# Self-attention of a fused transformer block: the shift of half of the scores moved from DMAs to VectorE and GpSimd, and a reciprocal taken on turned squares

## The chip, the cores and the metric

The program runs on one core of a Trainium2 chip. The metric is the device time of one execution in microseconds (us). Three runs of the kernel before gave a median of 2473.12 us (2465.09 to 2479.93).

The engines are named as in the profile: PE is TensorE (matmuls), PEld its weight loads, DVE is VectorE, ACT is ScalarE, POOL is GpSimd, SP is SyncE, which here only issues DMAs. SBUF is the on-chip memory and PSUM the memory into which matmuls write.

## The reference

A block of eight batches with 512 rows of 512 numbers goes through a cross-attention layer, then through a block of self-attention, a second cross-attention and an MLP. All is float32. Only the self-attention is touched here; it has 16 heads of width 32, and its queries and keys both have 512 positions:

```python
x_norm = modulate(_ln(x), shift_a, scale_a)
qkv = x_norm @ W_qkv + b_qkv
q, k, v = jnp.split(qkv, 3, axis=-1)
...
attn_w = jax.nn.softmax(jnp.einsum('bhqd,bhkd->bhqk', q, k) * scale, axis=-1)
attn_out = jnp.einsum('bhqk,bhkd->bhqd', attn_w, v)
...
attn_out = attn_out @ W_proj + b_proj
x = x + gate_a[:, None] * attn_out
```

## The kernel before

The program runs its stages one after the other: a setup, the first cross-attention (phase "x"), the self-attention (`self_phase`, phase "a", from about 430 us to about 1315 us of the profiled span), the second cross-attention ("c") and the MLP ("m"). In these stages every engine works through its instructions in the order in which the program lists them; no scheduler reorders them. So the place of a call in the loop is its place in the queue of its engine.

**Groups.** The self-attention works in 32 groups. One group is four heads of one batch: eight batches (`b`) times four sets of heads (`fc`, 0 to 3). A group holds its scores turned: keys lie on the 128 partitions and queries along the row, so a group has four key tiles `k` of 128 keys, each with four heads of 512 queries. Each key tile is held as two SBUF tiles `e[k][0]` and `e[k][1]` of 128 x 1024 numbers, two heads in each.

**The steps of one group**, with the lines of the profile:

- `scores(k)`: eight matmuls (L1177) write two PSUM tiles `sT`. ACT copies both into `e[k]` (L1195). DVE keeps a running maximum `mx` over the key tiles (L1197, two instructions for each of k = 1, 2, 3), which also reads PSUM. The PSUM tiles have two buffers, so the matmuls of tile k+1 wait until both readers of tile k are through.
- `maxima()`: DVE turns each of the four heads' maxima in 32 x 32 squares (L1208) and reduces them (L1209), into `part`.
- `spread()`: PE turns `part` (L1217), DVE reduces it to the negated maximum of every query and head (L1221), and SP stores these 8 KB to DRAM as `mxd` (L1226).
- `shift(k)`: two DMAs for each key tile (L1231), issued by POOL, read a row of `mxd` for all 128 partitions and add it to `e[k][0]` and `e[k][1]` on the way.
- `exp(k)`: ACT takes the exponent in place (L1240).
- `add_up(k)`: adds `e[k]` into `sum`, on POOL for k = 1 and 2, on DVE for k = 3 (L1247).
- `outputs(k)`: matmuls with the values (L1257) accumulate in PSUM.
- `total()` and `finish()`: PE sums over the partitions with a matrix of ones (L1268), so that `z_ps` holds the sum of each head in all of the 32 partitions that belong to it. DVE takes the reciprocal of all 128 x 512 numbers (L1275) and multiplies the output by it (L1278).

**The loop.** The steps of three groups are interleaved: in the round of group `g`, its successor `nxt` has its scores and maxima computed, `prev` has its last tiles finished and the group before that (`past`) is divided. `beside(b, fc)` gives each round four pieces of eight matmuls, `f[0]` to `f[3]`, made of queries, keys, values or the output projection of this or a neighbouring batch (L352, L360). DVE also does, in the rounds where they are due, the bias of the projection (`res_a`, L1145) and the statistics of the next layer norm (L253 and L254 in rounds fc = 3, L268 to L298 in rounds fc = 0). `flush` puts on POOL the product of a projected tile with its gate (L1148) and the DMA that adds it to the residual in DRAM (L1151).

The order of one round is therefore, for PE: scores 0, the turned maxima of `g`, the sums of `past`, `f[0]`, scores 1, outputs 2 of `prev`, `f[1]`, scores 2, outputs 3 of `prev`, half of `f[2]`, scores 3, its other half, outputs 0 of `g`, `f[3]`, outputs 1 of `g`. In round fc = 2 there are four more small pieces that turn x (L1098).

Of the kernel before, what the change touches and what calls it, by code (L numbers as in the profile page):

```python
# [11 lines left out]
F32 = mybir.dt.float32  # L12
I32 = mybir.dt.int32
AF = mybir.ActivationFunctionType
ALU = mybir.AluOpType
# [4 lines left out]
P = 128  # L20
# [10 lines left out]
def tile_pixart_block(ctx: ExitStack, tc: tile.TileContext, a: dict, out: bass.AP):  # L31
    nc = tc.nc
    x, ctx_in, cond = a["x"], a["ctx_1024"], a["cond_1024"]
    B, N, _ = x.shape
# [13 lines left out]
    small = ctx.enter_context(tc.tile_pool(name="small", bufs=4))  # L48

    def load_w(name, u, rows=False, pool=wpool, queue=nc.sync):  # L50

        t = pool.tile([P, KC, H], F32, tag="w", name=f"w_{name}_{u}")
        w = a[name]
        src = w[ts(u, H), :] if rows else w[:, ts(u, H)]
        queue.dma_start(out=t, in_=src.rearrange("(k p) f -> p k f", p=P))
        return t
# [135 lines left out]
    with tc.tile_pool(name="setup_ps", bufs=4, space=PSUM) as spp, tc.manual_schedule(  # L192
# [6 lines left out]
        for name, n in col_names:  # L199
            at = col_at[name]  # L200
            nc.gpsimd.dma_start(
                out=brow[at : at + n, :],
                in_=a[name][0 : n * P].rearrange("(c p) -> c p", p=P),
# [193 lines left out]
    with tc.tile_pool(name="ps_s", bufs=2, space=PSUM, reuse_waits="tile") as ps_s:  # L397
# [672 lines left out]
        def self_phase(w, bo_row, work, work_2, ctx_c):  # L1070
# [6 lines left out]
            SQ = 32  # L1077
            KQ = N // SQ
# [6 lines left out]
            def flush(part):  # L1085

                while later[part]:
                    later[part].popleft()()
# [6 lines left out]
            def transpose_x(b, k):  # L1095
                pt = ps_m.tile([P, H], F32, tag="m", name=f"lnT_ps_a{b}_{k}")
                for t in range(NT):
                    nc.tensor.transpose(pt[:, ts(t, P)], x_cur[:, t, ts(k, P)], ident)  # L1098
                o = work.tile([P, N], F32, tag="xnT", bufs=5, name=f"xnT_a{b}_{k}")
                nc.scalar.activation(  # L1100
                    o, pt, AF.Identity,
                    bias=mod_l1[:, k, b : b + 1], scale=mod_l1[:, KC + k, b : b + 1],
                )
                st[b]["xT"].append(o)
# [54 lines left out]
            class Group:  # L1159
# [53 lines left out]
                def spread(self):  # L1213


                    pt = ps_m.tile([P, H], F32, tag="m", name=f"mxT_ps_{self.nm}")
                    nc.tensor.transpose(  # L1217
                        pt[: 4 * KQ, :P], self.part.rearrange("p h c -> p (h c)"), ident
                    )
                    row = small.tile([4 * KQ, SQ], F32, tag="mxT", bufs=1, name=f"mxT_{self.nm}")  # L1220
                    nc.vector.tensor_reduce(  # L1221
                        row, pt[: 4 * KQ, :P].rearrange("c (g q) -> c q g", q=SQ), AX.X, ALU.max,
                        negate=True,
                    )
                    self.mxd = dram.tile([4, N], F32, tag="mx", bufs=4, name=f"mxd_{self.nm}")
                    nc.sync.dma_start(out=self.mxd.rearrange("h (c q) -> (h c) q", q=SQ), in_=row)  # L1226

                def shift(self, k):

                    for i in range(2):  # L1230
                        nc.gpsimd.dma_start(  # L1231
                            out=self.e[k][i].rearrange("p h n -> p (h n)"),
                            in_=self.mxd[2 * i : 2 * i + 2, :]
                            .rearrange("h n -> (h n)").partition_broadcast(P),
                            accum_op=ALU.add,
                        )

                def exp(self, k, halves=(0, 1)):
                    for i in halves:
# [32 lines left out]

                def finish(self):
                    r = work.tile([P, N], F32, tag="rz", bufs=1, name=f"rz_{self.nm}")
                    nc.vector.reciprocal(r, self.pz)  # L1275
                    o = work.tile([P, N], F32, tag="oT", bufs=6, name=f"oT_{self.nm}")
                    st[self.b]["o"].append(o)
                    return nc.vector.tensor_tensor(o, self.po, r, ALU.mult)  # L1278

            def beside(b, fc):  # L1280

                more = b + 1 < B
                none = iter(())
                if fc == 0:
                    return [values(b, 2), values(b, 3), queries(b, 2), keys(b, 2)]
                if fc == 1:
                    done = [project(b - 1, t) if b else none for t in range(2)]
                    return [queries(b, 3), done[0], keys(b, 3), done[1]]
                done = [project(b - 1, t) if b else none for t in (2, 3)]
                if fc == 2:  # L1290
                    return done + ([queries(b + 1, 0), keys(b + 1, 0)] if more else [none, none])
                return [values(b + 1, 0), values(b + 1, 1), queries(b + 1, 1), keys(b + 1, 1)]
# [20 lines left out]
            for n, g in enumerate(groups[:-1]):  # L1313
                b, fc = g.b, g.fc
                nxt = groups[n + 1]
                more = b + 1 < B
                f = beside(b, fc)
                turning = fc == 2 and more
                if fc == 3:
                    ln = normalise_x("a", b + 2, True) if b + 2 < B else iter(())  # L1320
                if not more and fc == 1:
                    ctx_c.w_k = load_w("L1_xcond_W_kvc", 0)
                if prev is not None:
                    prev.outputs(1)
                nxt.scores(0)
                g.spread()
                if past is not None:
                    past.total()
                    past.finish()
                if prev is not None:  # L1330
                    prev.add_up(2, [0])
                g.shift(0)
                if prev is not None:
                    prev.add_up(2, [1])
                    prev.exp(3, [0])
                for k in range(1, NT):
                    g.shift(k)
                flush(0)
                flush(1)
                if fc == 1 and more:  # L1340
                    next(ln)
                pump(f[0], 4)
                nxt.scores(1)
                if fc == 3 or (b, fc) == (0, 0):
                    next(ln, None)
                    next(ln, None)
                elif fc == 0 and more:
                    next(ln)
                if turning:
                    transpose_x(b + 1, 0)  # L1350
                if prev is not None:
                    prev.exp(3, [1])
                    prev.outputs(2)
                if fc == 1 and more:
                    next(ln)
                pump(f[1], 4)
                if fc == 1 and not more:
                    ctx_c.load()
                    ln = ctx_c.norm()
                if turning:  # L1360
                    transpose_x(b + 1, 1)
                nxt.scores(2)
                if turning:
                    transpose_x(b + 1, 2)
                if fc == 2 and not more:
                    next(ln)
                    next(ln)
                if prev is not None:
                    prev.add_up(3)
                if (b, fc) == (0, 0):  # L1370
                    next(ln)
                if prev is not None:
                    prev.outputs(3)
                if turning:
                    transpose_x(b + 1, 3)
                    if b + 2 < B:
                        load_x(b + 2)
                flush(0)
                flush(1)
                g.exp(0)  # L1380
                pump(f[2], 2)
                nxt.scores(3)
                pump(f[2], 2)
                g.exp(1)
                g.add_up(1)
                if fc == 2 and not more:
                    run(ln)
                nxt.maxima()
                g.outputs(0)
                pump(f[3], 4)  # L1390
                if fc == 2 and not more:
                    ctx_c.transpose()
                g.exp(2)
                past, prev = prev, g

            g = groups[-1]
# [6 lines left out]
            prev.exp(3)  # L1403
            for k in range(1, NT):
                g.shift(k)
            flush(0)
            flush(1)
            prev.outputs(2)
# [99 lines left out]
        with tc.tile_pool(name="work_a", bufs=2, reuse_waits="tile") as work, tc.tile_pool(  # L1508
            name="ps_a", bufs=2, space=PSUM, reuse_waits="tile"
        ) as ps_m, tc.tile_pool(  # L1510
            name="ps_o", bufs=2, space=PSUM, reuse_waits="tile"
# [28 lines left out]
    with tc.tile_pool(name="mlp", bufs=1, reuse_waits="tile") as mlp, tc.tile_pool(  # L1540
        name="mlp_w", bufs=MC // KC - 1, reuse_waits="tile"
    ) as mlp_w, tc.tile_pool(
        name="ps_q", bufs=6, space=PSUM, reuse_waits="tile"
    ) as ps_q, tc.tile_pool(
        name="ps_t", bufs=2, space=PSUM, reuse_waits="tile"
# [39 lines left out]
        SQ = 32  # L1585
# [216 lines left out]
        for c in range(2):  # L1802
            g, r, s = [mlp.tile([P, H2], F32, tag="xr", bufs=4, name=f"shift_{i}_{c}")[:B] for i in range(3)]
# [47 lines left out]
```

## Time and profile before

| | |
|---|---|
| median of 3 runs | 2473.12 us (2465.09 to 2479.93) |
| profiled execution | 2467.43 us, of which the span of the engines is 2465.6 us |
| busy over the span | PE 95%, PEld 61%, DVE 68%, ACT 47%, POOL 52% |
| TensorE clock granted, mean | 0.984 |
| busy from 909 to 1011 us (102 us, most of one batch of the self-attention) | PE 98.71, DVE 86.46, ACT 74.30, POOL 75.80 us |
| share of the 16 DMA engines in that stretch | 0.97, 187 GB/s |
| DMAs that shift the scores (L1231) | 256 of 512 KB, 11.6 us median from issue to landing |
| reciprocal of the sums (L1275) | 32 on DVE, 3357 ns each |

A row of a timeline gives the start in us, the duration, the engine, the line, the operation with output and inputs, the shape, the number of instructions merged into the row, and in brackets the idle time of the engine before it with what ended it. A matmul of 512 float32 columns appears as two instructions. POOL rows can overlap: an instruction's row may begin while DMA descriptors ahead of it on POOL are still being written.

### The profile page before, as it was taken

The page shows a single profiled execution, that of the slowest core. Times are in us where ns is not written, and L with a number is a line of the kernel's source. Part 1 is how long each engine was busy: PE and PEld are TensorE (multiplying, and loading weights), DVE is VectorE, ACT ScalarE, POOL GpSimd, SP SyncE. Part 2 cuts the span into 40 slices and gives each one's busy share as a digit, 9 for nine tenths or more (in the row PEclk, how much of TensorE's full clock was granted, in tenths as well). Part 3 has the DMA queues.
Part 4 walks back from the last instruction along what each step waited for, and adds up shares of the span by engine and source line. Part 5 has one row for each costly group of instructions (what it writes and reads, how often), then busy time and mean ns, then how long its engine had stood idle before and what let it go on. Part 6 is the DMA issues. An engine that isn't in the chain of part 4 may idle for free.

```text
span 2465.6 us, 44805 instructions
## 1 busy us (share of the span) xinstructions
PE 2344.2 (95%) x17737; PEld 1508.8 (61%) x17737; DVE 1665.7 (68%) x2861; ACT 1168.7 (47%) x2045; POOL 1271.8 (52%) x1325
## 2 busy tenths in 40 slices
PE   8889998899999999999988899998999999999998
PEld 4667776323333333333324677777888888888887
DVE  3677774588888888888755787767555546555552
ACT  1456663577677777777653566642122121121120
POOL 2467774367786777867664567755302312213122
PEclk9899999999999999999999799999999999999999
DMA  7456666498999999999995224433422322223210
GB/s 247 128 130 145 123 131 117 89 189 171 193 191 182 197 173 194 192 181 180 201 205 148 78 64 89 80 70 104 89 40 60 73 53 64 58 54 78 44 51 26
DMA packets 145848, 300.94 MB, mean 122 GB/s; under 512 B 17573, under 2 KB 48437, under 8 KB 145125
## 3 DMA queue, kind: packets, MB, share of 16 engines
q0 software_dynamic: 60192, 176.24, 40.3%
q1 hardware_dynamic: 80148, 111.33, 15.7%
q10 hardware_dynamic: 5296, 10.50, 1.2%
q8 instruction: 140, 2.29, 0.4%
q14 instruction: 72, 0.58, 0.1%
HBM read 254.28 MB, written 53.17 MB: 125 GB/s over the span
## 4 chain that ended last, share of the span: by engine, by line
PE 76%; DVE 11%; DMA 5%; ACT 4%; issue 2%; POOL 1%; SPq 0%; POOLq 0%; ACTq 0%; DVEq 0%
PE q_ps_y L1652 16%; PE q_ps_h L1652 15%; PE proj_ps_a L360 4%; PE sT_a L1177 4%; DMA e_a<-mxd_a 3%; PE sa_ps_qc L554 3%; DVE mx_a L1197 3%; PE v_ps L360 3%; PE q_ps_a L352 3%; PE o_ps_a L1257 2%; PE sa_ps_qx L554 2%; PE k_ps_a L352 2%; PE sa_ps_oc L554 2%; PE sa_ps_ox L554 2%; PE s_c L873 2%
## 5 line engine op out<-in xcount | busy, mean ns | idle before, releaser
L1231 POOL DMA_DIRECT2D e_a<-mxd_a x256 | 250.4, 2061 | 157.3 <-DMA mxd_a<-mxT_a 148.4
L1240 ACT ACTIVATE e_a<-e_a 128x1024 f32<-128x1024 f32 x256 | 265.4, 1057 | 85.5 <-DMA e_a<-mxd_a 85.2
L1195 ACT COPY e_a<-sT_a 128x1024 f32<-128x1024 f32 x256 | 254.9, 1009 | 95.6 <-DVE mx_a L1197 47.0
L1247 POOL TENSOR_TENSOR sum_a<-e_a,e_a 128x1024 f32<-128x1024 f32 x64 | 153.6, 2444 | 101.3 <-ACT e_a L1240 100.7
L1685 ACT ACTIVATE hT<-hT,bcol 128x512 f32<-128x512 f32 x128 | 91.8, 721 | 239.5 <-DVE hT L1660 231.6
L180 POOL DMA_DIRECT2D x_m<-in_L_xcond_b_cproj_dram x32 | 29.9, 1364 | 326.0 <-DMA x_m<-xa 326.0
L1247 POOL TENSOR_TENSOR sum_a<-sum_a,e_a 128x1024 f32<-128x1024 f32 x64 | 172.3, 2702 | 2.7 <-ACT e_a L1240 2.7
L1197 DVE TENSOR_TENSOR mx_a<-sT_a,mx_a 128x1024 f32<-128x1024 f32 x128 | 150.8, 1218 | 31.0 <-PE sT_a L1177 29.3
L1177 PE MATMUL sT_a<-qT_a,kT_a 32*128 32x512 f32 x1024 | 150.9, 643 | 12.6 <-ACT e_a L1195 11.0
L1752 POOL TENSOR_TENSOR res_m<-res_m,gate_m 128x256 f32<-128x256 f32 x64 | 49.9, 779 | 206.2 <-DVE res_m L1660 206.0
L1257 PE MATMUL o_ps_a<-e_a,v 128*32 128x512 f32 x1024 | 146.6, 608 | 7.0 <-ACT e_a L1240 7.0
L852 POOL TENSOR_TENSOR p_c<-p_c,sm_c 128x616 f32<-128x616 f32 x64 | 84.1, 1438 | 96.3 <-ACT xnT_c L341 42.0
L1652 PE MATMUL q_ps_h<-x_m,w_L_xcond_W_mlp 128*128 128x256 f32 x512 | 131.4, 379 | 0.0
L1652 PE MATMUL q_ps_h<-xT_m,w_L_xcond_W_mlp 128*128 128x256 f32 x512 | 131.4, 379 | 0.0
L352 PE MATMUL q_ps_a<-xnT_a,w_L_xcond_W_qkv 128*128 128x512 f32 x256 | 124.1, 613 | 6.9 <-ACT xnT_a L1100 6.9
L1275 DVE RECIPROCAL rz_a<-z_ps_a 128x512 f32<-128x512 f32 x32 | 107.4, 3357 | 31.4 <-PE z_ps_a L1268 31.4
L1652 PE MATMUL q_ps_h<-x_m,w_s 128*128 128x256 f32 x512 | 121.6, 380 | 6.7 <-DVE w_s L1575 6.0
L352 PE MATMUL k_ps_a<-xnT_a,w_L_xcond_W_qkv 128*128 128x512 f32 x256 | 120.4, 608 | 0.0
L360 PE MATMUL v_ps<-w_L_xcond_W_qkv,xnT_a 128*128 128x512 f32 x256 | 120.0, 612 | 0.0
L360 PE MATMUL proj_ps_a<-w_L_xcond_W_proj,oT_a 128*128 128x512 f32 x256 | 117.9, 605 | 1.4 <-DVE oT_a L1278 1.4
L1652 PE MATMUL q_ps_y<-w_L_xcond_W_mlp,h_s 128*128 128x256 f32 x512 | 113.1, 379 | 0.0
L1652 PE MATMUL q_ps_y<-w_L_xcond_W_mlp,hT 128*128 128x256 f32 x512 | 113.1, 379 | 0.0
(427 smaller groups left out, 5418.9 us busy)
## 6 DMA issues: line engine op xcount, KB each, us to landing
e_a<-mxd_a POOLq DMA_DIRECT2D x256, 512.0 KB, 11.6
xa<-in_x_dram SPq DMA_DIRECT2D x32, 256.0 KB
xa<-in_L_xcond_bp_dram POOLq DMA_DIRECT2D x32, 256.0 KB, 5.7
xa<-res_x POOLq DMA_DIRECT2D x32, 256.0 KB, 5.9
xa<-res_a POOLq DMA_DIRECT2D x32, 256.0 KB, 14.9
w_L_xcond_W_mlp<-in_L_xcond_W_mlp_dram SPq DMA_DIRECT2D x8, 1024.0 KB
xa<-res_c POOLq DMA_DIRECT2D x32, 256.0 KB, 5.1
x_m<-xa SPq DMA_DIRECT2D x32, 256.0 KB
```

The source lines that it names most:

```text
L352: nc.tensor.matmul(ps, lhsT=w[:, k, ts(j, P)], rhs=xT[k], start=(k == 0), stop=(k == KC - 1))
L360: nc.tensor.matmul(ps, lhsT=xT[k][:, cols], rhs=w[:, k, :], start=(k == 0), stop=(k == KC - 1))
L554: nc.tensor.matmul(ps, lhsT=self.lhs[i][:, k], rhs=self.rhs[i][:, k], start=(first and k == 0), stop=(k == 1), skip_group_check=not first,)
L1177: nc.tensor.matmul(sc[h // 2][:, h % 2, :], lhsT=kT[ts(h, HD), ts(k, P)], rhs=qT[ts(h, HD), :], start=True, stop=True,)
L1195: nc.scalar.copy(self.e[k][i], sc[i])
L1197: nc.vector.tensor_tensor(self.mx[1 - i], sc[1 - i], self.e[0][1 - i] if k == 1 else self.mx[1 - i], ALU.max,)
L1231: nc.gpsimd.dma_start(out=self.e[k][i].rearrange("p h n -> p (h n)"), in_=self.mxd[2 * i : 2 * i + 2, :] .rearrange("h n -> (h n)").partit ...
L1240: nc.scalar.activation(self.e[k][i], self.e[k][i], AF.Exp)
L1247: engine.tensor_tensor(sum_i, self.e[0][i] if k == 1 else sum_i, self.e[k][i], ALU.add)
L1257: nc.tensor.matmul(self.po[ts(h, HD), :], lhsT=vt[:, self.fc * P + h * HD : self.fc * P + (h + 1) * HD], rhs=self.e[k][h // 2][:, h % 2, : ...
L1275: nc.vector.reciprocal(r, self.pz)
L1652: nc.tensor.matmul(self.banks[n][:, half], lhsT=lhsT, rhs=rhs, start=(k == 0), stop=(k == len(pairs) - 1),)
```

## The change

Three things change, all in the self-attention.

1. `spread()` gets a second DMA on SP's queue. It waits for the store of `mxd` and reads the first two heads' rows back for all 128 partitions, into an SBUF tile `mxb` of 128 x 1024 (one buffer, 512 KB in all).
2. `shift(k)` now issues one DMA, for `e[k][1]`. The half `e[k][0]` is shifted by `shift_first(k, engine)`, an addition of `mxb` with both inputs in SBUF: on POOL for k = 2 and 3, right after the flushes that follow the shift DMAs; on DVE for k = 0 ahead of the maxima of scores 2, and for k = 1 behind `prev.add_up(3)`, ahead of the maxima of scores 3.
3. `finish()` turns the sums in 32 x 32 squares on DVE, takes the reciprocal of the 16 columns of 128 numbers that then hold every sum once, and turns them back with a broadcast input. Three instructions stand where one was.

```diff
@@ spread
                     nc.sync.dma_start(out=self.mxd.rearrange("h (c q) -> (h c) q", q=SQ), in_=row)
+                    self.mxb = work.tile([P, 2, N], F32, tag="mxb", bufs=1, name=f"mxb_{self.nm}")
+                    nc.sync.dma_start(
+                        out=self.mxb.rearrange("p h n -> p (h n)"),
+                        in_=self.mxd[0:2, :].rearrange("h n -> (h n)").partition_broadcast(P),
+                    )
@@ shift
-                    for i in range(2):
-                        nc.gpsimd.dma_start(
-                            out=self.e[k][i].rearrange("p h n -> p (h n)"),
-                            in_=self.mxd[2 * i : 2 * i + 2, :]
-                            .rearrange("h n -> (h n)").partition_broadcast(P),
-                            accum_op=ALU.add,
-                        )
+                    nc.gpsimd.dma_start(
+                        out=self.e[k][1].rearrange("p h n -> p (h n)"),
+                        in_=self.mxd[2:4, :].rearrange("h n -> (h n)").partition_broadcast(P),
+                        accum_op=ALU.add,
+                    )
+
+                def shift_first(self, k, engine):
+
+                    engine.tensor_tensor(self.e[k][0], self.e[k][0], self.mxb, ALU.add)
@@ finish
                     r = work.tile([P, N], F32, tag="rz", bufs=1, name=f"rz_{self.nm}")
-                    nc.vector.reciprocal(r, self.pz)
+                    part_z = small.tile([P, KQ], F32, tag="zp", bufs=1, name=f"z_{self.nm}")
+                    nc.vector.transpose(r, self.pz)
+                    nc.vector.reciprocal(
+                        part_z, r.rearrange("p (c k) -> p c k", k=SQ)[:, :, 0]
+                    )
+                    nc.vector.transpose(
+                        r.rearrange("p (c k) -> p c k", k=SQ),
+                        part_z.unsqueeze(2).to_broadcast([P, KQ, SQ]),
+                    )
@@ the loop over the groups
                 flush(0)
                 flush(1)
+                for k in (2, 3):
+                    g.shift_first(k, nc.gpsimd)
...
                 if turning:
                     transpose_x(b + 1, 1)
+                g.shift_first(0, nc.vector)
                 nxt.scores(2)
...
                 if prev is not None:
                     prev.add_up(3)
+                g.shift_first(1, nc.vector)
@@ after the loop, the last group
             for k in range(1, NT):
                 g.shift(k)
+            for k in range(2):
+                g.shift_first(k, nc.vector)
+            for k in (2, 3):
+                g.shift_first(k, nc.gpsimd)
             flush(0)
             flush(1)
```

## The prediction

> **What bounds the kernel now.** The page shows a full PE over the span, so I looked at the self-attention alone: busy time by stretch, then who waits for the DMAs, then the order of events in one round on DVE and PE. First a stretch of 102 us, nearly one batch, since the batches repeat every 102.7 us (the first projection of a batch starts at 703.2, 805.86, 908.71, 1011.47 and 1114.08 in the chain of waits). Columns: stretch, length, busy PE, PEld, DVE, ACT, POOL, then clock, DMA share, GB/s.
>
> ```profile
> 909.00:1011.00 102.00, 98.71 (x436) 32.72 (x434) 86.46 (x101) 74.30 (x84) 75.80 (x56) 1.00 0.97 187
> ```
>
> Two things look like the bound: PE with 3.3 us idle, and the DMA engines at 97%. The shift DMAs are what fills the latter: the POOL queue took 40.3% of 2465.6 us for 176.24 MB, 5.64 us per MB on all 16 engines, so 2.96 us for each of 0.524 MB and 23.7 us for the eight of a group whose round lasts 25.7 us. But who waits for them?
>
> ```profile
> DMA to landing us min/median/max: 4.9/11.6/21.5
> ```
> ```profile
> PE q_ps_a L352 <- ACT xnT_a L1100: 4.9, 5, 1.0
> PE mxT_ps_a L1217 <- DVE part_a L1209: 4.2, 13, 0.5
> PE sT_a L1177 <- ACT e_a L1195: 3.9, 4, 1.2
> PE z_ps_a L1268 <- DVE res_a L1145: 1.5, 5, 0.3
> PE o_ps_a L1257 <- ACT e_a L1240: 0.2, 1, 0.2
> ```
>
> These are all waits of PE from 700 to 1180 us (total us, times, longest): 14.7 us in 480. Only the last, 0.2 us, is for shifted scores. In 13 of 19 rounds PE waits for `part`, the end of DVE's maxima. So DVE is level with PE; how, the order shows. DVE in a round fc = 0, and PE in the same round:
>
> ```profile
> 971.95 0.69 DVE L1278 TENSOR_TENSOR oT_a<-o_ps_a,rz_a 128x512 f32<-128x512 f32 x1
> 973.33 2.36 DVE L1197 TENSOR_TENSOR mx_a<-sT_a,e_a 128x1024 f32<-128x1024 f32 x2 [0.69 <-PE sT_a L1177]
> 975.60 2.42 DVE L268 TENSOR_SCALAR lnv_a<-mv_a 128x4 f32<-128x4 f32 x1
> ...
> 980.22 2.35 DVE L1197 TENSOR_TENSOR mx_a<-sT_a,mx_a 128x1024 f32<-128x1024 f32 x2
> 982.48 2.35 DVE L1247 TENSOR_TENSOR sum_a<-sum_a,e_a 128x1024 f32<-128x1024 f32 x2
> 984.75 2.35 DVE L1197 TENSOR_TENSOR mx_a<-sT_a,mx_a 128x1024 f32<-128x1024 f32 x2
> 987.01 0.70 DVE L1208 STREAM_TRANSPOSE tu_a<-mx_a 128x512 f32<-128x512 f32 x1
> ```
> ```profile
> 972.02 1.14 PE L1177 MATMUL sT_a<-qT_a,kT_a 32*128 32x512 f32 x8
> ...
> 992.89 0.30 PE L1217 MATMUL mxT_ps_a<-ident,part_a 128*64 128x128 f32 x1 [0.54 <-DVE part_a L1209]
> ```
>
> From 973.33 on DVE has no gap until `part` (992.84), and PE then waits for it. Before 973.33 DVE waits for PE's scores 1, which PE reaches about 6 us after the turned maxima whatever DVE does (sums 1.0, f[0] 3.63, scores 1.07). So the round is one loop: turned maxima, 6 us of PE, then DVE's chain. What is put on DVE behind scores 1 lengthens the round; what is saved ahead of scores 1 turns into idle time.
>
> **The change part by part.**
>
> *Reciprocal* (ahead of scores 1). One of 3.36 us goes; two square turns at 0.71 (row L1208) and a reciprocal of 16 columns, 3357/512 = 6.6 ns a column, 0.1 us plus a start of about 0.1, come: 1.6 us. It saves 1.75 us a group, and in the row above 0.69 us of idle already lie behind it. In the steady loop it is worth nothing; at the very end PE waits 1.43 us for this chain, and I count 1.4 there. If the broadcast input made the last turn twice as long, that too would be hidden.
>
> *Shift DMAs.* Four of eight go and one plain one comes: SP's queue took 15.7% of the span for 111.33 MB, 1.8 us for 0.524 MB. So 4 x 2.96 + 1.8 = 13.7 us of 25.7. Its worth in the loop is bounded by PE's 0.2 us. At the ends of the stage there is more: `o_ps` waits 5.0 us and `sT` 1.5 us from 1130 on, and 2.0 us near 501. I take 8 of these 8.5; with the 1.4, -9 us (between 0 and -15, as copies of other waits there may follow).
>
> *`mxb`.* It cannot start before `mxd` is in DRAM. The first store, with idle DMAs, took 2.3 us (459.32 to 461.58, where POOL starts); today's later ones take about 6.3 (967.5 to 973.79) behind the queue of shifts, which will be gone by then. So about 2.7 us after the turned maxima are reduced (call that t = 0), then 0.5 to issue and 4.9 (the shortest landing of the same size) to 11.6 (the median one): t = 8 to 15. I take 8, the row with free DMA engines. The readers come at t = 9 on POOL and 11 to 13 on DVE; cover is 1 us and 3 us. With 15 DVE would stand for 2 to 4 us with the maxima, PSUM and scores behind it. On SP only the gate's load queues behind, needed 10 us later.
>
> *POOL.* Four DMA issues of 1.0 us go, two additions of 2.35 us (row of `sum_a`, alone) come: +0.7 us a group of 25.7, where it is busy 19 and waits some 4 us for `mxd` and up to 5 for exponents. Hidden.
>
> *DVE.* Two additions with both inputs in SBUF. The `sum_a` row is the same instruction: 1218 ns alone, 2.27 us for two, so 1.135 each, 2.27 a group, all of it behind scores 1. By round:
> - fc = 0 and fc = 3: no gap, +2.27 each.
> - fc = 1: a gap of 0.43 us behind `res_a`, +0.7 +1.13 = 1.85.
> - fc = 2: gaps of 0.87 and 0.52 us and PE a little behind, +0.6.
>
> A batch: 7.0 us. Seven batches less one round fc = 3: 7 x 7.0 - 2.3 = 47 us. In the last batch and the round before it there is no layer norm; DVE idles 3.3 us before scores 2's maxima and PE comes 0.7 us or more behind `part`: 0.
>
> *The two engines against each other.* Rows in which DVE was slow beside POOL:
>
> ```profile
> L1247 DVE TENSOR_TENSOR sum_a<-sum_a,e_a x64: 1211/1218/3359, 495.2 to 1293.1; 128x1024 f32<-128x1024 f32 x64
> L268 DVE TENSOR_SCALAR lnv_a<-mv_a x7: 160/2531/2762, 473.1 to 1078.1; 128x4 f32<-128x4 f32 x7
> ```
>
> (Shortest, median, longest.) The longest addition ran while POOL was in an addition of its own, and L268, 160 ns by itself, sat beside one in six of its seven runs. So one meeting costs DVE 2.1 to 2.4 us. The new POOL additions run from t = 9 to 14 (11 to 16 with a flush); DVE's shift 0 is due at t = 11 to 13 and its sums at 14 to 17. They do meet, and who is first is open: 0 to 2.4 us a round, while L268 may get its 2.4 us back since POOL's present addition moves forward with `mxd` (-14 in all). Over 27 rounds -14 to +65; I take 0.9 a round, +24, between the 0 of DVE first and the 2.4 of POOL first.
>
> The Trainium skill, page "SBUF — State Buffer", section "Who interferes with whom", says that a DVE instruction with two SBUF inputs and a GpSimd instruction that reads SBUF exclude each other for a whole instruction, and that the one issued second blocks. Both new kinds of addition are of that form, so the rule speaks against this change; by it alone, with POOL always first and one block a round, the term would be 27 x 2.35 = 63 us in place of 24.
>
> *Sum.* 47 + 24 - 9 = +62 us. Against the profiled execution, 2467.4 us: 2529. The median is 5.7 us higher and within the spread of the three runs; I leave that out.
>
> **The rivals.**
>
> *The DMAs were the bound after all* (faster). For it: 97% share, ACT waits 36.4 us in 480 for shifted scores. Against it: PE waits 0.2 us for what ACT makes of them. If DVE's two additions were wholly hidden, all of PE's waits but those for x (4.9) could go, 9.8 in 480 us, 14 us over the loop, and 15 at the ends: 2438. It decides if the wait for `part` does not grow. 9%.
>
> *It cancels* (within 0.5%). PE is the true bound by a margin that I do not see, DVE adds some 0.4 us a round, the ends give 9: about 2469. That the reciprocal's 1.75 us count after all is part of it. 6%.
>
> *`mxb` lands late or POOL always wins* (slower still). 2.35 us of blocking or 2 to 3 us of waiting in each of 27 rounds: 47 + 65 - 4 = +108, 2575. 20%.
>
> My forecast, DVE's chain with some blocking: 65%.
>
> **How the numbers follow.** Low end: the chain alone with everything at the ends gained, 47 - 14 - 9 = +24, 2491, taken as 2490; the first two rivals, 15%, lie below it. High end: past the 2575 of the third rival, as blocking and waiting can add up (27 x 2.35 more would give 2638); at 2590 I leave out a quarter of its 20%. That is 2 in 10 outside. About 0.5% (12 us) is the least that can be told from no change. Faster 0.09, same 0.06, slower 0.65 + 0.20 = 0.85.
>
> **What would show it.** Right: PE's wait for `part` grows from 0.2-0.5 us to 2-3 us in rounds fc = 0, 1 and 3, the batches repeat every 110-114 us, DVE idles more ahead of the maxima of scores 1, DMA share falls to about 0.55, `mxd` lands in under 3 us, some DVE additions take 2 us or more. Wrong: batches still at 102.7 us or shorter, or DVE's first addition waiting for `mxb`.

## The result, and the profile after

The changed kernel takes 2609.68 us (median of four runs, 2602.98 to 2619.83), the kernel before 2470.11 us beside it: a ratio of 1.0559, 95% interval 1.0529 to 1.0589, so 139.6 us slower. The forecast was slower by 62 us, and the time lies above its range. The direction held, the size did not.

The profiled execution took 2619.83 us with a span of 2618.1 us, 152.5 us over the span before. First the stretch of 100 us that answers to the one shown of before (stretch, length, busy PE, PEld, DVE, ACT, POOL, clock, DMA share, GB/s).

```profile
1000.00:1100.00 100.00, 85.82 (x355) 28.66 (x351) 83.28 (x102) 58.26 (x67) 62.74 (x38) 0.91 0.48 98
```

The DMA engines went from 97% to 48%, as the prediction had it, and nothing is gained by it. PE, which idled 3.3 us in 102, now idles 14.2 in 100. What it waits for, again from 700 to 1180 us (total us, times, longest):

```profile
PE sT_a L1177 <- ACT e_a L1195: 35.6, 11, 4.5
PE q_ps_a L352 <- ACT xnT_a L1100: 29.7, 4, 8.6
PE mxT_ps_a L1217 <- DVE part_a L1209: 2.3, 2, 1.2
PE z_ps_a L1275 <- DVE res_a L1145: 0.9, 3, 0.3
```

The 14.7 us of waits became 68.5. Both large rows name ACT, but ACT is 58% busy: it stands itself behind DVE (the page puts 186.6 us of the idle time before the copies L1195 down to the maxima L1197). So one looks at DVE's instructions that read SBUF alone. First the groups that matter, on POOL and DVE, shortest, median and longest in ns:

```profile
L1243 POOL TENSOR_TENSOR e_a<-e_a,mxb_a x64: 2347/3638/3727, 470.7 to 1422.8; 128x1024 f32<-128x1024 f32 x64
L1243 DVE TENSOR_TENSOR e_a<-e_a,mxb_a x64: 1193/1216/9347, 476.8 to 1427.4; 128x1024 f32<-128x1024 f32 x64
```
```profile
L268 DVE TENSOR_SCALAR lnv_a<-mv_a x7: 160/5032/5195, 481.3 to 1201.6; 128x4 f32<-128x4 f32 x7
```

The median of DVE's new addition is the 1.2 us that was counted, its longest 9.35 us. POOL's rows overlap, so 3.6 us is not the length of its addition: the second of a pair starts 2.3 us after the first. L268 adds a constant to four numbers a partition and has one input; it took 2.5 us in the kernel before and takes 5.0 now. Round fc = 2 shows the longest common case, on DVE, POOL, ACT and PE in turn:

```profile
1018.19 7.12 DVE L1243 TENSOR_TENSOR e_a<-e_a,mxb_a 128x1024 f32<-128x1024 f32 x1
1025.23 2.34 DVE L1197 TENSOR_TENSOR mx_a<-sT_a,mx_a 128x1024 f32<-128x1024 f32 x2
```
```profile
1016.83 4.96 POOL L1243 TENSOR_TENSOR e_a<-e_a,mxb_a 128x1024 f32<-128x1024 f32 x2
1021.46 2.75 POOL L1148 TENSOR_TENSOR res_a<-res_a,gate_a 128x512 f32<-128x512 f32 x2
```
```profile
1026.53 1.01 ACT L1195 COPY e_a<-sT_a 128x1024 f32<-128x1024 f32 x1 [6.38 <-DVE mx_a L1197]
...
1027.44 1.45 ACT L1100 ACTIVATE xnT_a<-lnT_ps_a,mod_l 128x512 f32<-128x512 f32 x2
```
```profile
1028.27 3.78 PE L352 MATMUL q_ps_a<-xnT_a,w_L_xcond_W_qkv 128*128 128x512 f32 x4 [7.06 <-ACT xnT_a L1100]
...
1033.15 1.98 PE L352 MATMUL q_ps_a<-xnT_a,w_L_xcond_W_qkv 128*128 128x512 f32 x4
```

DVE's addition is issued at 1018.19, 1.4 us into POOL's first one. It does not get in after that instruction, nor after the second, nor after the first product: POOL's train of four ends at 1024.21, and DVE ends 1.1 us later, the length of its own work. It waited out the whole train. Behind it stand the maxima of scores 2; behind those ACT's copy, for 6.38 us; and behind that copy, in ACT's queue, the last two pieces of xnT, which have nothing to do with the scores and whose inputs PE had finished at 1021.2. PE stands for 7.06 us.

To see where each kernel loses, I use the time from one group's turned maxima on PE (L1217) to the next, by round, as a mean over the rounds of groups 4 to 26. "Batch" is the sum of the four (differences in the last digit are rounding). Each row is one execution. e1 has the same median as before and a batch 1.2 us longer, so a difference of that size says little:

| kernel | fc = 0 | fc = 1 | fc = 2 | fc = 3 | batch | ratio to before (95%) |
|---|---|---|---|---|---|---|
| before | 25.83 | 24.48 | 27.83 | 24.61 | 102.75 | |
| e1, the turned reciprocal alone | 25.85 | 25.11 | 28.37 | 24.60 | 103.93 | 0.9999 (0.9986 to 1.0011) |
| after | 30.97 | 28.54 | 35.99 | 28.91 | 124.41 | 1.0559 (1.0529 to 1.0589) |
| e3, two reductions on VectorE | 26.07 | 26.30 | 29.56 | 26.53 | 108.46 | 1.011 (1.009 to 1.013) |
| e4, VectorE's half alone | 25.73 | 26.21 | 28.00 | 26.55 | 106.49 | 1.0029 (1.0017 to 1.0041) |
| e5, GpSimd's half alone | 32.49 | 26.76 | 30.56 | 25.85 | 115.66 | 1.0317 (1.0299 to 1.0336) |
| e7, the layer norm moved | 24.66 | 25.13 | 27.83 | 25.22 | 102.84 | 0.9975 (0.9962 to 0.9989) |
| e8, e4 with unrelated GpSimd reads | 32.23 | 28.36 | 31.12 | 27.69 | 119.40 | 1.0406 (1.0380 to 1.0432) |
| e9, e4 with GpSimd fills | 26.33 | 26.77 | 29.32 | 26.55 | 108.97 | 1.0092 (1.0063 to 1.0121) |
| e10, the train parted | 31.12 | 28.94 | 29.74 | 29.07 | 118.87 | 1.0414 (1.0381 to 1.0447) |
| e11, e4 with VectorE reordered | 25.66 | 24.47 | 28.26 | 24.47 | 102.87 | 0.9941 (0.9920 to 0.9963) |
| e12, after with the layer norm away | 32.83 | 28.23 | 36.53 | 28.33 | 125.91 | 1.0596 (1.0564 to 1.0628) |

### The profile page after: what moved, and what is told of

It reads as the page before. It is cut to its first block, busy times and chain, and to the rows that moved or that the text cites. A ratio compares the mean times of both kernels' runs of the same rounds, so it can differ in the third digit from the quotient of the medians.

```text
span 2618.1 us, 44758 instructions
## 1 busy us (share of the span) xinstructions
PE 2397.3 (92%) x17737; PEld 1526.8 (58%) x17737; DVE 1783.4 (68%) x2989; ACT 1165.4 (45%) x2045; POOL 1302.4 (50%) x1261
## 4 chain that ended last, share of the span: by engine, by line
PE 73%; DVE 14%; issue 6%; ACT 4%; POOL 2%; DMA 1%; SPq 0%; POOLq 0%; DVEq 0%; ACTq 0%
PE q_ps_y L1675 15%; PE q_ps_h L1675 14%; PE q_ps_a L352 4%; PE proj_ps_a L360 4%; DVE mx_a L1197 3%; PE sT_a L1177 3%; PE k_ps_a L352 3%; PE o_ps_a L1264 2%; PE v_ps L360 2%; PE sa_ps_qc L554 2%; PE sa_ps_qx L554 2%; PE sa_ps_oc L554 2%; PE sa_ps_ox L554 2%; PE s_c L873 2%; PE s_x L873 2%
## 5 line engine op out<-in xcount | busy, mean ns | idle before, releaser
L1195 ACT COPY e_a<-sT_a 128x1024 f32<-128x1024 f32 x256 | 256.0, 1012 | 281.1 <-DVE mx_a L1197 186.6
L1247 ACT ACTIVATE e_a<-e_a 128x1024 f32<-128x1024 f32 x256 | 259.0, 1056 | 6.9 <-DVE e_a L1243 6.9
L1177 PE MATMUL sT_a<-qT_a,kT_a 32*128 32x512 f32 x1024 | 160.6, 691 | 79.2 <-ACT e_a L1195 77.6
L352 PE MATMUL q_ps_a<-xnT_a,w_L_xcond_W_qkv 128*128 128x512 f32 x256 | 152.5, 733 | 46.2 <-ACT xnT_a L1100 46.2
L1243 POOL TENSOR_TENSOR e_a<-e_a,mxb_a 128x1024 f32<-128x1024 f32 x64 | 180.4, 3293 | 0.4 <-DMA mxb_a<-mxd_a 0.3
L1243 DVE TENSOR_TENSOR e_a<-e_a,mxb_a 128x1024 f32<-128x1024 f32 x64 | 167.6, 2620 | 5.0 <-DMA mxb_a<-mxd_a 5.0
L1197 DVE TENSOR_TENSOR mx_a<-sT_a,mx_a 128x1024 f32<-128x1024 f32 x128 | 150.1, 1211 | 18.9 <-PE sT_a L1177 18.4
L1254 POOL TENSOR_TENSOR sum_a<-sum_a,e_a 128x1024 f32<-128x1024 f32 x64 | 160.3, 2511 | 4.9 <-ACT e_a L1247 4.8
L1235 POOL DMA_DIRECT2D e_a<-mxd_a x128 | 123.8, 1364 | 56.1 <-DMA mxd_a<-mxT_a 42.5
L1177 PEld LDWEIGHTS sT_a<-qT_a,kT_a 32*128 32x128 f32 x1024 | 43.5, 193 | 182.6 <-ACT e_a L1195 100.2
L352 PEld LDWEIGHTS q_ps_a<-xnT_a,w_L_xcond_W_qkv 128*128 128x128 f32 x256 | 53.6, 229 | 136.0 <-issue 82.3
L1197 DVE TENSOR_TENSOR mx_a<-sT_a,e_a 128x1024 f32<-128x1024 f32 x64 | 75.3, 1218 | 73.8 <-PE sT_a L1177 73.8
```

The costliest lines, as they stand in the source:

```text
L352: nc.tensor.matmul(ps, lhsT=w[:, k, ts(j, P)], rhs=xT[k], start=(k == 0), stop=(k == KC - 1))
L1177: nc.tensor.matmul(sc[h // 2][:, h % 2, :], lhsT=kT[ts(h, HD), ts(k, P)], rhs=qT[ts(h, HD), :], start=True, stop=True,)
L1195: nc.scalar.copy(self.e[k][i], sc[i])
L1197: nc.vector.tensor_tensor(self.mx[1 - i], sc[1 - i], self.e[0][1 - i] if k == 1 else self.mx[1 - i], ALU.max,)
L1235: nc.gpsimd.dma_start(out=self.e[k][1].rearrange("p h n -> p (h n)"), in_=self.mxd[2:4, :].rearrange("h n -> (h n)").partition_broadcast(P ...
L1243: engine.tensor_tensor(self.e[k][0], self.e[k][0], self.mxb, ALU.add)
```

## The experiments

The runs fall in three lots: which part of the change costs the time (1 to 5), whether the clock does (6), and what the meeting of the two engines is and where it can be put (7 to 12).

**1. The turned reciprocal alone**, in the kernel before.

```diff
-                    nc.vector.reciprocal(r, self.pz)
+                    nc.vector.transpose(r, self.pz)
+                    nc.vector.reciprocal(part_z, ...)      # 16 columns
+                    nc.vector.transpose(..., part_z ... to_broadcast)
```

> The kernel before with the turned reciprocal alone. All theories: the 1.75 us that DVE saves in a group lie ahead of its wait for scores 1, so the loop does not move; only the last group's chain at the end may gain. Expected 0 to -5 us against before. If it gains 20 us or more, the loop was bound by DVE ahead of scores 1 and the forecast's reading of the loop is wrong.

2473.48 us against 2473.98, ratio 0.9999 (0.9986 to 1.0011). The three instructions take 0.72, 0.25 and 0.71 us in place of 3.36, and it is worth nothing: the saving lies ahead of scores 1, where DVE waits for PE. The broadcast input does not make the last turn longer. In the profiled execution the loop (first to last turned maxima) is 806.7 us against 797.7, and 14 of DVE's sums are held up beside GpSimd there, 8 before; the medians show nothing of it, and whether the earlier place of DVE's work makes these meetings was not tried.

**2. The shift alone**, with the old reciprocal: `finish()` as before, the rest as changed.

> The whole change without the turned reciprocal (one reciprocal of 3.36 us as before). All theories: the loss is in the shift, so +130 to +150 us against before, like the whole change. If it is clearly above 150, the turned reciprocal had hidden a part of the loss.

2622.43 us, ratio 1.0603 (1.0575 to 1.0631). The shift carries the whole loss. Whether the reciprocal saves a little inside the changed kernel is not settled, since the two intervals overlap.

**3. Two dummy instructions on VectorE**, in the kernel before, at the places of its two additions. They have one SBUF input.

```diff
+                def load_dve(self, k):
+                    t = small.tile([P, 2], F32, tag="dl", ...)
+                    nc.vector.tensor_reduce(t, w_o[:, 0:2, :], AX.X, ALU.max)
...
+                g.load_dve(0)
                 nxt.scores(2)
...
+                g.load_dve(1)
```

> The kernel before, with two reductions of a constant 128x1024 tile on DVE in each round, at the two places where the change puts DVE's additions; they have one SBUF input and their result is not used. It prices the longer chain without any meeting of DVE and POOL. Theory 1 (DVE's additions stand behind whole trains of POOL instructions, and that makes most of the loss): +45 to +65 us. Theory 2 (the 2.3 us in the chain are enough, enlarged by PE's lower clock and by ACT's queue): +100 us or more.

2501.65 us, ratio 1.011 (1.009 to 1.013): +27.7 us for two instructions of 1.21 us, below what either theory gave. L268 gave some time back: its median is 0.40 us here and 2.53 before. PE's wait for `part` from 700 to 1110 us:

```profile
PE mxT_ps_a L1217 <- DVE part_a L1209: 16.9, 15, 1.2
```

That is the signature which the prediction gave for its chain, a wait for `part` in most rounds. DVE's work at these two places does set the round.

**4. VectorE's half alone**: GpSimd's two additions go back to accumulating DMAs.

```diff
-                    nc.gpsimd.dma_start(out=self.e[k][1]..., in_=self.mxd[2:4, :]..., accum_op=ALU.add)
+                    for i in (0, 1) if k > 1 else (1,):
+                        nc.gpsimd.dma_start(out=self.e[k][i]..., in_=self.mxd[2 * i : 2 * i + 2, :]..., accum_op=ALU.add)
...
-                for k in (2, 3):
-                    g.shift_first(k, nc.gpsimd)
```

> The change with POOL's two additions taken back: key tiles 0 and 1 are shifted by DVE as in the change, tiles 2 and 3 by DMAs as before. DVE's instructions are those of the change, POOL's additions are gone. Theory 1: +45 to +75 us, near the run with the two reductions, and DVE's additions at 1.2 us nearly all. Theory 2: +100 us or more, near the whole change.

2481.38 us, ratio 1.0029 (1.0017 to 1.0041), +7.4 us, again below what either theory gave. DVE's addition and L268:

```profile
L1245 DVE TENSOR_TENSOR e_a<-e_a,mxb_a x64: 1191/1217/1481, 471.1 to 1292.2; 128x1024 f32<-128x1024 f32 x64
```
```profile
L268 DVE TENSOR_SCALAR lnv_a<-mv_a x7: 158/159/205, 475.6 to 1101.5; 128x4 f32<-128x4 f32 x7
```

Without POOL's additions none of DVE's new additions is longer than 1.48 us, and L268 is back at 159 ns. So 132 of the 139.6 us belong to two GpSimd additions a round.

**5. GpSimd's half alone**: the mirror of experiment 4, with DVE's additions back on DMAs.

> The change with DVE's two additions taken back: tiles 2 and 3 are shifted by POOL as in the change, tiles 0 and 1 by DMAs as before. Theory 1 (trains): POOL's longer train now meets only DVE's sums of tile 3 and the layer-norm scalars of round fc = 0, so +10 to +45 us. Theory 2 (chain): nothing is added to DVE's chain, so within 10 us of before.

2552.31 us, ratio 1.0317 (1.0299 to 1.0336), +78.7 us, far over what I expected. GpSimd's additions need none of VectorE's new ones to do harm; they find L268 and the sums that were always there (one sum took 11.57 us). DVE and POOL in a round fc = 0:

```profile
1029.98 6.90 DVE L268 TENSOR_SCALAR lnv_a<-mv_a 128x4 f32<-128x4 f32 x1
```
```profile
1030.12 6.71 POOL L1245 TENSOR_TENSOR e_a<-e_a,mxb_a 128x1024 f32<-128x1024 f32 x2
```

**6. PE kept busy through its waits**: the changed kernel with repeated first matmuls of a piece ahead of scores 3 (fc 0, 1 and 3) and the last transposes of x repeated six times more (fc 2). The rival reason was that PE's gaps let its clock fall, 0.984 to 0.951 in the mean, as in the row above where four matmuls take 3.78 us after the 7.06 us stall and 1.98 us later; the granted clock was 0.50 from 1028.27 to 1032.00 us and 1.00 from 1033.15 on. The Trainium skill's page "TensorE: Matmul & The Clock Gate", section "Part 1: The HAM clock gate (the "warmup" mystery)", says that the array falls to half its clock after an idle window of about 3.4 us; this row, after 7.06 us, agrees.

> The change, with idle stretches of PE filled: two matmuls are done once more ahead of scores 3 in rounds fc = 0, 1 and 3 (same inputs, overwritten by the true ones), and the last transposes of x six times more in round fc = 2. PE gets about 1.7 us more work in three rounds and 3.4 us in the fourth. If the slow matmuls behind the stalls (q of 4 rows at 3.5 to 3.7 us where 1.92 is usual) come from the stall itself, the granted clock goes back towards 1.0 and the time falls by 15 to 45 us against the whole change, though PE does more. If they do not, it stays the same or gets up to 10 us longer.

2612.42 us, ratio 1.0565 (1.0544 to 1.0587); the granted clock was 0.973 in the mean, and in 700 to 1100 us it went from 0.91 to 0.97. The time did not move, and a batch came to 123.44 us against 124.41. So the lower clock, which came from the waits, is no large part of the 139.6 us. As the run adds matmuls to win the clock back, it does not tell a small cost of the clock from none.

**7. The layer norm's pieces moved ahead of scores 1**, in the kernel before with the turned reciprocal.

```diff
                     past.finish()
+                if fc == 3:
+                    next(ln, None)
+                    next(ln, None)
+                elif fc == 0 and b and more:
+                    next(ln)
...
                 nxt.scores(1)
-                if fc == 3 or (b, fc) == (0, 0):
+                if (b, fc) == (0, 0):
...
-                elif fc == 0 and more:
-                    next(ln)
```

> The kernel before with the turned reciprocal, and the layer-norm pieces of DVE moved ahead of its wait for scores 1: the statistics in rounds fc = 3, the scalars in rounds fc = 0. That takes 3.3 and 4.6 us out of DVE's chain in those rounds, and adds about 1 us ahead of the maxima of scores 1 in round fc = 3. If the chain is what PE waits for, PE's waits of 0.5 to 0.8 us for it go there: -6 to -15 us against before. If PE is the bound by itself, 0.

2466.23 us against 2473.63, ratio 0.9975 (0.9962 to 0.9989). Round fc = 0 goes from 25.83 to 24.66 us (25.85 in experiment 1, which has the same reciprocal), so there DVE's chain was what the round waited for. Round fc = 3, from which 3.3 us were taken too, did not get shorter: 24.61 before, 25.22 now. From the second batch on no round of fc = 0, 1 or 3 is shorter than 24.47 us before, here or in experiment 11, so that looks like the length of PE's own work. The 7.4 us are at the low end of what was expected.

**8. Unrelated reads by GpSimd**: experiment 4 with two additions at the place of GpSimd's, which read the output weights and write a tile that nobody reads.

```diff
+                    t = work.tile([P, 2, 448], F32, tag="pw", bufs=1, ...)
+                    for _ in range(2):
+                        nc.gpsimd.tensor_tensor(t, w_o[:, 0:2, :448], w_o[:, 2:4, :448], ALU.add)
```

> The changed kernel with both of GpSimd's additions of a round moved to the accumulating DMAs (as in the run with VectorE's half alone, +7.4 us), and in their place two GpSimd additions of two slices of the output weights (128x896 float32 each) into a scratch tile that nobody reads. This work is bound to nothing in the round by its data; what it shares with the additions is only the engine, its place in the queue and that it reads SBUF. Theory 1 (VectorE waits out GpSimd's SBUF instructions): the 18 us a batch come back almost in full, 12 to 18 us a batch, +90 to +140 us in all over the kernel before, and VectorE's addition of fc 2 again takes over 4 us. Theory 2 (the additions hold the round up by their data: the shifted scores of parts 2 and 3 come later to ScalarE's exponentials): unrelated work costs only GpSimd's own delay, +7 to +30 us in all, and VectorE's additions stay at 1.2 us.

2574.49 us, ratio 1.0406 (1.0380 to 1.0432). A batch is 12.91 us longer than in experiment 4, of the 17.92 that the real additions cost. Theory 1 holds in its lower part, but for VectorE's addition of fc = 2, which stays at 1.2 us in all but the first and the last batch; there the sums are held up. Theory 2 does not hold: most of the harm is done without the additions' data. What the other 5 us are is not shown, since the real additions are also longer (2.3 against 2.08 us) and give DVE no turn. Here it is let in between:

```profile
1056.08 2.20 DVE L268 TENSOR_SCALAR lnv_a<-mv_a 128x4 f32<-128x4 f32 x1
1058.31 2.03 DVE L270 TENSOR_SCALAR lny_a<-lnv_a 128x4 int32<-128x4 int32 x1
...
1060.46 2.04 DVE L275 TENSOR_TENSOR lnt_a<-lny_a 128x4 f32<-128x4 f32 x1
```

Three tiny instructions pay some 2 us each, in place of one that pays 5.

**9. Fills in place of reads**: the same with `for _ in range(4): nc.gpsimd.memset(t, 0.0)`.

> As the run with GpSimd reading the weights, but GpSimd's work at that place is four fills of the scratch tile with zeros (128x896 float32 each): it keeps GpSimd as busy, writes SBUF and reads none. If it is the reads with which GpSimd shuts VectorE out, this stays at +5 to +25 us over the kernel before, VectorE's additions at 1.2 us; if writes or simply a busy GpSimd do it, +60 to +140 us as with the reads.

2497.15 us, ratio 1.0092 (1.0063 to 1.0121); a batch is 2.5 us longer than in experiment 4. POOL is busy for 4 x 0.85 us instead of 2 x 2.08 us alone, so four fifths as long, for a fifth of the harm. DVE's addition stays short but for ten of 64:

```profile
L1251 DVE TENSOR_TENSOR e_a<-e_a,mxb_a x64: 1191/1217/2298, 472.0 to 1305.8; 128x1024 f32<-128x1024 f32 x64
```

The ten, and twelve of DVE's sums, are all those over 1.3 us, and each stood beside a GpSimd instruction that reads SBUF, mostly the gate products (POOL, then DVE):

```profile
1064.83 3.52 POOL L1148 TENSOR_TENSOR res_a<-res_a,gate_a 128x512 f32<-128x512 f32 x2
```
```profile
1067.14 2.29 DVE L1251 TENSOR_TENSOR e_a<-e_a,mxb_a 128x1024 f32<-128x1024 f32 x1
```

Another 35 of these additions and sums ran beside fills and no such instruction, and none of them took over 1.22 us. So it is not that a fill is shorter: most of the harm comes from GpSimd's instructions that read SBUF, not from a busy GpSimd.

**10. The train parted**: one of GpSimd's additions between its DMA issues, the other behind the flushes.

```diff
-                for k in range(1, NT):
-                    g.shift(k)
+                g.shift(1)
+                g.shift(2)
+                g.shift_first(2, nc.gpsimd)
+                g.shift(3)
                 flush(0)
                 flush(1)
-                for k in (2, 3):
-                    g.shift_first(k, nc.gpsimd)
+                g.shift_first(3, nc.gpsimd)
```

> The changed kernel with GpSimd's two additions of a round parted: the one of part 2 behind the DMA issue of part 2, then the issue of part 3 and the gates and stores, then the addition of part 3. Both additions stay. Theory 1a (VectorE waits until GpSimd's unbroken train of instructions is over): with the train cut, VectorE's 7.1 us addition of fc 2 falls to 2 to 5 us and the loss from +139 us to +60 to +120 us. Theory 1b (each instruction shuts VectorE out for its own length only): the number of meetings is as it was, the loss stays at +130 to +150 us, and the longest VectorE addition stays under two instructions of GpSimd wherever two follow one another.

2580.09 us, ratio 1.0414 (1.0381 to 1.0447). Nearly all that comes back is in round fc = 2, 35.99 to 29.74 us; the other rounds stay. In round fc = 0 only a DMA issue stands between the two additions, and it opens no gap (POOL, then DVE):

```profile
1056.18 2.60 POOL L1243 TENSOR_TENSOR e_a<-e_a,mxb_a 128x1024 f32<-128x1024 f32 x1
1058.49 1.14 POOL L1235 DMA_DIRECT2D e_a<-mxd_a  x1
1059.09 2.92 POOL L1243 TENSOR_TENSOR e_a<-e_a,mxb_a 128x1024 f32<-128x1024 f32 x1
```
```profile
1056.96 5.08 DVE L268 TENSOR_SCALAR lnv_a<-mv_a 128x4 f32<-128x4 f32 x1
```

L268 ends with the second addition. In round fc = 2 a product and its store lie between as well; DVE's first addition is through before the second train, which then holds the sums, for 2.6 us in place of the 5.9 before:

```profile
1006.06 4.97 DVE L1254 TENSOR_TENSOR sum_a<-sum_a,e_a 128x1024 f32<-128x1024 f32 x2
```

So theory 1a holds where the train was really cut, which one DMA issue did not do.

**11. VectorE's half, reordered**: experiment 4 with both additions right behind scores 1 and the layer norm as in experiment 7.

```diff
                 nxt.scores(1)
+                g.shift_first(0, nc.vector)
+                g.shift_first(1, nc.vector)
```

> The kernel with VectorE's half of the shift alone (+7.4 us over the kernel before) with two moves in VectorE's order: both additions stand right behind scores 1 of the next head group, and the layer norm's pieces of fc 0 and 3 ahead of scores 1, as in the run that moved them alone (-7.4 us). If VectorE's order is what the +7.4 us was made of, this comes to -5 to -20 us against the kernel before; if the additions' 2 x 1.2 us of work lie on VectorE's chain wherever they stand, 0 to +10 us.

2460.47 us against 2476.7, ratio 0.9941 (0.9920 to 0.9963): the fastest version here, faster than before beyond its interval, though by 0.6%. The loop is as long as before (102.87 us a batch), although both additions stand behind scores 1. In rounds fc = 0 and 3 the layer norm's pieces made room for them; in fc = 1 they fill a wait of DVE for PE's projection. Before, and in this run:

```profile
797.93 0.69 DVE L1145 TENSOR_TENSOR res_a<-proj_ps_a,row_L_xcond_b_proj 128x512 f32<-128x512 f32 x1 [2.15 <-PE proj_ps_a L360]
```
```profile
795.45 2.35 DVE L1245 TENSOR_TENSOR e_a<-e_a,mxb_a 128x1024 f32<-128x1024 f32 x2
797.72 0.68 DVE L1145 TENSOR_TENSOR res_a<-proj_ps_a,row_L_xcond_b_proj 128x512 f32<-128x512 f32 x1
```

That round takes 24.47 us, as before, and 26.21 in experiment 4, where both additions come behind this wait. From the last turned maxima to the end of the span the run takes 1198.4 us, before 1209.2: the 10.8 us lie behind the loop. 8.7 of them are there by the end of the self-attention's last projection. PE's waits for exponents (2.1 us) and for the last reciprocal's product (1.4 us), both gone, are a part; the rest is not split up.

**12. The layer norm moved away in the changed kernel**, with the edit of experiment 7.

> The changed kernel with the layer norm's pieces of fc 0 and 3 taken out of the place where they stand beside GpSimd's additions and put right behind the finish of the outputs, as in the run that moved them in the kernel before (-7.4 us there). In fc 0 the first of them (L268) waits about 5 us for GpSimd's two additions. Theory A (the wait belongs to GpSimd's additions and falls on whatever VectorE instruction with two SBUF reads or on its first SBUF instruction comes next): the wait moves on to VectorE's own addition, fc 0 becomes like fc 3 (31.0 to about 29 us), and the whole comes to +110 to +135 us over the kernel before, against +139.6 for the changed kernel. Theory B (it is a price of the place of L268 alone): fc 0 loses all of its 5 us, and with it the whole comes to +85 to +105 us.

2624.7 us, ratio 1.0596 (1.0564 to 1.0628): above both ranges. Theory B falls. Theory A is right that the wait moves on and wrong about where to: the layer norm's chain is 13 instructions long, and another of them caught GpSimd's train (DVE, then POOL):

```profile
1086.69 0.16 DVE L275 TENSOR_TENSOR lnt_a<-lny_a 128x4 f32<-128x4 f32 x1
1086.89 6.17 DVE L276 TENSOR_TENSOR lnt_a<-lnt_a,lnv_a 128x4 f32<-128x4 f32 x1
```
```profile
1087.06 5.96 POOL L1243 TENSOR_TENSOR e_a<-e_a,mxb_a 128x1024 f32<-128x1024 f32 x2
```

An instruction of 0.16 us took 6.17, and now the maxima of scores 1 stand behind it: round fc = 0 grew from 30.97 to 32.83 us.

## Why the prediction was right in direction and wrong in size

The spans of three profiled executions split the loss in the prediction's own terms. Experiment 4 holds everything but GpSimd's additions. One execution each: the spans of e4 and before lie 15.6 us apart where the medians lie 7.4 apart, so some 8 us of the first two rows are chance.

| term | predicted | measured |
|---|---|---|
| DVE's chain, with L268's 2.4 us given back | 47 - 14 = +33 | e4 minus before, first to last turned maxima: 824.1 - 797.7 = +26.4 |
| ends of the stage | -9 | e4 minus before, the rest of the span: -10.8 |
| the two engines against each other, without L268's return | 24 + 14 = +38 | after minus e4, whole span: 2618.1 - 2481.2 = +136.9 |
| sum | +62 | +152.5 (medians: +139.6) |

**The step that failed is the term for the two engines against each other**: "0 to 2.4 us a round", of which I took 0.9. In the loop it was 17.92 us a batch, 4.5 a round, nearly twice the upper bound. Three things were wrong in it.

- The price of a meeting was one GpSimd instruction. It is what is left of the train: 5.0 us for L268 in fc = 0, 7.1 us for the addition in fc = 2, where two gate products joined the train, 3.2 and 2.9 us for the additions of fc = 1 and 3. Above each one's own time that is 4.9 + 5.9 + 2.0 + 1.7 = 14.5 of the 17.92 us. The bound came from a kernel in which the longest meetings took 2.1 to 2.4 us, and was carried over to one whose change puts two such instructions side by side.
- L268 was to get its wait back, since POOL's old addition moves forward. It did move (L268 is at 159 ns in experiment 4), and POOL's new ones came into its place. I had followed DVE's new instructions to their meetings, and not the old ones. Experiment 5 shows how much that alone weighs: +78.7 us.
- DVE's wait does not end at DVE. In fc = 2 ACT's copy stood behind the maxima and the pieces of xnT behind the copy, so PE lost the time ahead of the projection. Of the 7.99 us that this round lost to GpSimd, 5.9 are DVE's wait; that the other 2.1 are this knock-on is read from the one round shown, not measured apart.

**The chain was right for the two places that the change uses**, and somewhat too large: +26.4 by the spans and nearer +18 by the medians (7.4 + 10.8), for +33. By round, experiment 4 minus before gives -0.10, +1.73, +0.17 and +1.94 us, for 2.27 - 2.37 = -0.1, 1.85, 0.6 and 2.27. Round fc = 0 is even only because L268's wait paid for it. Its rule, that what is put on DVE behind scores 1 lengthens the round, was too wide: in fc = 1 DVE waits 2.15 us for the projection behind scores 1, and in experiment 11 two additions fit in there at no cost. **The reciprocal** was worth nothing alone, as counted, and **the ends** are there in experiments 4 and 11; in the changed kernel itself they were eaten (+3.3 us outside the loop instead of -9). **`mxb`** was in time: DVE waited 5.0 us for it in the whole run.

Of the signs that were named, the DMA share (0.48), DVE's idle time ahead of scores 1's maxima (0.69 us before, 2.3 in round fc = 0 now), the landing of `mxd` (POOL issues the first shift 2.2 us after the reduced maxima, median, 6.0 before) and the additions over 2 us came. The batches went past the 110 to 114 us that were named, to 124.4. The wait for `part` did not: PE waits 2.3 us for it in all, from 700 to 1180 us, since DVE is held so long in the middle of the round that PE stops earlier, at the scores or at the projection of the queries.

**The rivals.** That the DMAs were the bound falls with a share of 48% and no gain. That it cancels falls with +139.6 us. "`mxb` lands late or POOL always wins", +108, was the nearest in size: its second half happened, and at more than its price.

The Trainium skill's rule, page "SBUF — State Buffer", section "Who interferes with whom", was the better guide: by it the term was 63 us in place of 24. The runs agree that two SBUF inputs on DVE are shut out by GpSimd's reads of SBUF (experiment 9 against 8), while the maxima, which read PSUM, keep their 2.34 us a pair. They show more than the form that the prediction took from the page: L268, with one SBUF input, is held as well (5.0 us). And the waiting side was let in not after one whole instruction of the other, but after up to four (7.12 us).

## What to carry to other kernels

Before giving GpSimd an elementwise instruction on SBUF, list what VectorE does on SBUF alone, the tiny instructions too, in the whole time that GpSimd's unbroken run of such instructions can take, look in a profile which of them are held up, and price a meeting at the rest of that run, not of one instruction. Ask next what stands behind the waiting instruction on its own engine and behind its reader on the next one. Two additions on VectorE, in places where it waited or that were cleared for them, cost the loop nothing here (experiment 11), while the same number on GpSimd, which was half idle, cost 132 us.

## What the runs showed of the hardware that was not expected

VectorE waited behind GpSimd through runs of two and four instructions with no turn of its own (5.0, 6.2, 7.1 us). The longest waits, 9.35 us in the changed kernel and 11.57 in experiment 5, go through GpSimd's DMA issues too, and in experiment 10 a DMA issue between two additions gave VectorE no turn either (5.08 us). It is not always so: in experiment 12 L268 was let in when GpSimd's sum ended at 1085.7 us, ahead of three issues. In experiment 8 it did get turns of some 2 us; there both GpSimd instructions write one tile, so the second depends on the first. Whether that is the reason was not tried. An instruction on 128 x 4 numbers is held as long as one on 128 x 1024.

Not every instruction on SBUF is held. L268 and, in experiment 8, L270 have one SBUF input and wait (5.0 and 2.03 us). The statistics of the layer norm also have one, stand beside the same additions in rounds fc = 3 of the changed kernel, and never take over 0.69 us:

```profile
L253 DVE BATCH_NORM_STATS2 st_a<-x_a x28: 659/661/685, 473.6 to 1175.7; 128x6 f32<-128x512 f32 x28
```

What parts the two kinds was not tried.
